# Turning the normalised rows by GpSimd and two-byte DMA transposes instead of TensorE, in six down stages of a macaron block

## The chip, the cores and the metric

The kernel runs on one NeuronCore of a Trainium2 chip. The metric is the device time of one execution in microseconds (us). The core has TensorE (PE in the profile; PEld is its loading of weights), VectorE (DVE), ScalarE (ACT), GpSimd (POOL) and SyncE (SP), which here issues nearly all DMAs. Each engine works through its own queue in order.

## The reference

The input is u, 2 x 1024 rows of 1024 numbers, in float32. The block is a feed-forward layer, an S4 layer (a long convolution along the row) and a second feed-forward layer, each on normalised rows and added to its input:

```
x = x + 0.5 * ffn(layernorm(x))
x = x + s4(layernorm(x))
x = x + 0.5 * ffn(layernorm(x))
ffn(x) = (silu(x @ Wg) * (x @ Wu)) @ Wd
```

Wg and Wu are 1024 x 2752, Wd is 2752 x 1024. They come as 4-bit integers with a scale and a zero point for every 128 rows. Both feed-forward layers use the same weights.

## The kernel before

The 2048 rows are cut into four blocks of 512 (TB), each of four tiles of 128 rows (NT = 4). With two feed-forward layers for each block there are eight jobs, in the order of the list `JOBS`: (block, layer) = (0,1), (1,1), (0,3), (1,3), (2,1), (3,1), (2,3), (3,3). Job j has two stages. `gate_up` takes 64 steps and computes silu(x Wg) * (x Wu); `down` takes 44 steps and multiplies by Wd. The last phases of a job overlap with the preparation of the next through hooks: lists of small functions, `up` and `dn`, that are called at a given step of the stage, before that step's matmuls are written. A scheduler then lays out each engine's queue; where `in_order_of_writing` wraps a hook, its instructions on the named engines keep the order in which they were written.

**Weights.** The integers minus their zero points were written to DRAM as bytes at the start. Every step needs one weight tile. `load_bytes` fetches its bytes by a DMA on SyncE (L627 for gate/up, L634 for down; written 4 steps ahead, 6 buffers), `make_weights` casts them to float32 on GpSimd (L643; written 3 steps ahead, 5 buffers). In a down step PE does eight matmuls of 128 x 512 (L758): four columns of the output, each with hidden values as a high part hh and a low part hl. After each step the sums in PSUM are scaled by the ratio of neighbouring scales, two of four by ScalarE (L665) and two by VectorE (L667). The products hh and hl of the last gate/up steps are still made by GpSimd (L727, L729) when the down stage begins.

**Rows into columns.** `gate_up` multiplies by the normalised rows with the features on partitions. It needs them in two pieces, named xTh (float32, 8 chunks x 512 rows) and xTl (float16, what the rounding of xTh left over). In the down stage of job j the pieces of job j + 1 are prepared, for its four row tiles t in turn:

- `normalized` (L221, VectorE): (x - mean) * 1/deviation, 128 x 1024, at step 1 + 4t.
- `turn` at steps 2 + 4t and 4 + 4t, for one half of 512 columns each: four PE transposes of 128 x 128 into a PSUM bank named pt (`turned`, L228), ScalarE copies them into xTh (L250), VectorE writes the difference as xTl (L251).

```
ps = turned(n, f"pt_{b}_{k}_{t}_{half}")
...
nc.scalar.copy(hi, ps)
nc.vector.tensor_tensor(lo, ps, hi.bitcast(F32), ALU.subtract)
```

In job 0 alone the copy goes to a buffer and GpSimd makes both pieces (L246 to L248), at steps that begin at 9. The pieces have one buffer each: the next job's are written while the down stage runs, after the present job's gate/up stage has read its own.

**Rows of the result.** From step 21 of a down stage `load_x` reloads the block's four row tiles from DRAM, and `back` (L780, L782) transposes the first half of the result by PE and adds it, at steps 26, 30, 34 and 38; the other half follows in the next gate/up stage. Row tiles of 128 x 1024 float32 of every kind share ten buffers (`t4`). Tiles g and hf have three buffers each and are otherwise used in gate/up stages.

Of the kernel before, what the change touches and what calls it, by code (L numbers as in the profile page):

```python
# [9 lines left out]
F32 = mybir.dt.float32  # L10
BF16 = mybir.dt.bfloat16
F16 = mybir.dt.float16
# [4 lines left out]
F32R = mybir.dt.float32r  # L17
AF = mybir.ActivationFunctionType
ALU = mybir.AluOpType
AX = mybir.AxisListType  # L20
ET = mybir.EngineType
# [3 lines left out]
P = 128  # L25
HID = 1024
INTER = 2752
TOK = 2048
TB = 512
NT = TB // P  # L30
NC = HID // P
# [24 lines left out]
def macaron_s4_kernel(  # L56
# [31 lines left out]
    nc = tc.nc  # L88
# [7 lines left out]
    xtpool = ctx.enter_context(tc.tile_pool(name="xT", bufs=1))  # L96
# [4 lines left out]
    gpool = ctx.enter_context(tc.tile_pool(name="g", bufs=3))  # L101
    hfpool = ctx.enter_context(tc.tile_pool(name="hf", bufs=3))
# [27 lines left out]
    def t4(name):  # L130
        return xpool.tile([P, HID], F32, tag="x", name=name)
# [9 lines left out]
    def in_order_of_writing(f, *engines):  # L141

        start = len(nc.cur_bb.bb.instructions)
        got = f()
        written = list(nc.cur_bb.bb.instructions)
        for e in engines:
            last = next((i for i in reversed(written[:start]) if i.engine == e), None)
            for ins in written[start:]:
                if ins.engine == e:
                    if last is not None:  # L150
                        tc.add_manual_dep(
                            ins,
                            last.name,
                            mybir.DependencyInfo(
                                mybir.DependencyClass.NoSync, mybir.DependencyReason.DATA
                            ),
                            reason="order of writing",
                        )
                    last = ins
        return got  # L160


    x = {}
    ln = {}

    def load_x(b, src):
        x[b] = []
        for t in range(NT):
            xt = t4(f"x_{b}_{t}")
            nc.sync.dma_start(xt, src[t])  # L170
            x[b].append(xt)

    def rows_of(dram, b):
        return [dram[bass.ds(b * TB + t * P, P), :] for t in range(NT)]

    def moments(b, k):
        for _ in moments_by_tile(b, k):
            pass

    def moments_by_tile(b, k):  # L180

        name = f"{b}_{k}"
        stats = small.tile([P, NT, 2, 6], F32, tag="stats", name=f"stats_{name}")
        mv = small.tile([P, NT, 2], F32, tag="mv", name=f"mv_{name}")
        for t in range(NT):
            for i in range(2):
                nc.vector.bn_stats(stats[:, t, i, :], x[b][t][:, bass.ts(i, 512)])  # L187
            nc.vector.bn_aggr(mv[:, t, :], stats[:, t, :, :].rearrange("p a s -> p (a s)"))
            yield
        guess(b, k, mv)  # L190
# [13 lines left out]
    def deviations(b, k, factor=1.0):  # L204


        mv, ve, r = ln.pop(b)
        e = small.tile([P, NT], F32, tag="e", name=f"e_{b}_{k}")
        for three in (3.0, 12.0, 768.0):
            nc.vector.tensor_tensor(e, r, r, ALU.mult)  # L210
            nc.vector.tensor_tensor(e, e, ve, ALU.mult)
            nc.vector.scalar_tensor_tensor(r, e, three, r, ALU.subtract, ALU.mult)
        nc.vector.tensor_scalar(r, r, -factor / 8192, None, ALU.mult)
        for t in range(NT):
            ln[b, t] = (mv[:, t, 0:1], r[:, t : t + 1], k)
        return r

    def normalized(b, t):
        m, r, k = ln[b, t]
        n = t4(f"xn_{b}_{k}_{t}")  # L220
        nc.vector.tensor_scalar(n, x[b][t], m, r, ALU.subtract, ALU.mult)  # L221
        return n

    def turned(n, name):

        ps = bank(name)
        for k in range(4):
            nc.tensor.transpose(ps[:, bass.ts(k, P)], n[:, bass.ts(k, P)], ident)  # L228
        return ps.rearrange("p (c t) -> p c t", c=4)


    pieces = {}

    def turn(b, t, n, half, by_pool=False):
        k = ln[b, t][2]
        if b not in pieces:
            pieces[b] = [
                xtpool.tile([P, NC, TB], dt, tag=f"xT{w}", name=f"xT{w}_{b}_{k}")
                for w, dt in (("h", F32R), ("l", F16))
            ]  # L240
        hi, lo = (a[:, 4 * half : 4 * half + 4, bass.ts(t, P)] for a in pieces[b])
        ps = turned(n, f"pt_{b}_{k}_{t}_{half}")
        if by_pool:
            both = gpool.tile([P, TB], F32, tag="g", name=f"turn_{b}_{k}_{t}_{half}")
            both = both.rearrange("p (c t) -> p c t", c=4)
            nc.scalar.copy(both, ps)  # L246
            nc.gpsimd.tensor_copy(hi, both)
            nc.gpsimd.tensor_tensor(lo, both, hi.bitcast(F32), ALU.subtract)  # L248
        else:
            nc.scalar.copy(hi, ps)  # L250
            nc.vector.tensor_tensor(lo, ps, hi.bitcast(F32), ALU.subtract)  # L251

# [275 lines left out]
    def in_pieces(at, hooks_and_steps, pieces):  # L530

        held = {}

        def piece(last):
            def step():
                if not held:
                    held[0] = pieces()
                for _ in held[0]:
                    if not last:
                        break  # L540

            in_order_of_writing(step, ET.DVE)

        for i, (hooks, s) in enumerate(hooks_and_steps):
            last = i == len(hooks_and_steps) - 1
            at(hooks, s, lambda last=last: piece(last))
# [114 lines left out]
    h = {}  # L661
# [128 lines left out]
    after = const.tile([P, 4, P], F32, tag="after", name="after")  # L790
# [227 lines left out]
    def s4_toeplitz():  # L1018

        rows, turn, whole = t4("s4_rows"), t4("s4_turn")[:, :P], t4("s4_whole")  # L1020
        nc.gpsimd.memset(turn, 0.0)
        nc.gpsimd.affine_select(
            out=turn,
            in_=turn,
            pattern=[[1, P]],
# [327 lines left out]
    def fast():  # L1353
        for j, (b, k) in enumerate(JOBS):
            prev = JOBS[j - 1] if j else None
            after = JOBS[j + 1] if j + 1 < len(JOBS) else None
            up, dn = {}, {}

            def at(hooks, s, f):
                hooks.setdefault(s, []).append(f)  # L1360

            if prev:
# [3 lines left out]
                if pk == 1:  # L1366
                    late = 34 if j == 1 else 0
# [51 lines left out]
            if j == 1:  # L1419
                tables = s4_tables()  # L1420
                for i in range(S4_PIECES):
                    piece = lambda: in_order_of_writing(lambda: next(tables, None), ET.DVE)
# [3 lines left out]
            if after:  # L1426
                ab, ak = after
                if ak == 1:
                    at(up, 55 if j == 0 else 6, lambda: load_x(ab, rows_of(u, ab)))
                    if j == 0:  # L1430
                        steps = [(dn, d) for d in range(3, 8)]
                        in_pieces(at, steps, lambda: moments_by_tile(ab, 1))
                        newton = lambda: deviations(ab, 1, LIFT)
                        at(dn, 8, lambda: in_order_of_writing(newton, ET.DVE))
                    else:
                        both = lambda: moments(ab, 1)
                        at(up, 44, lambda: in_order_of_writing(both, ET.DVE))
                        at(up, 45, lambda: deviations(ab, 1, LIFT))
                an = {}

                pool = j == 0

                def anorm(t):
                    an[t] = normalized(ab, t)

                o = 9 if j == 0 else 0
                for t in range(NT):
                    at(dn, o + 1 + 4 * t, lambda t=t: anorm(t))
                    at(dn, o + 2 + 4 * t, lambda t=t: turn(ab, t, an[t][:, :512], 0, by_pool=pool))
                    at(dn, o + 4 + 4 * t, lambda t=t: turn(ab, t, an[t][:, 512:], 1, by_pool=pool))  # L1450
# [6 lines left out]
        b = JOBS[-1][0]  # L1457
# [116 lines left out]
    srow_next, zeros_down = in_order_of_writing(start, *STARTING, ET.PE)  # L1574
    x.pop(0)
    fast()
    x.clear()
    other = nc.values_load(flag)
# [84 lines left out]
```

## Time and profile before

| | |
|---|---|
| three runs | 2132.9, 2134.52, 2134.49 us; median 2134.49 |
| profiled execution | 2136.97 us, span from first to last instruction 2135.1 us |
| granted TensorE clock | 0.997 |
| busy share of the span | PE 98%, DVE 80%, ACT 67%, POOL 50% |
| DMA | 132.14 MB, mean 62 GB/s |
| down stages of jobs 1 to 6 | 86.2, 85.5, 85.3, 85.6, 85.5, 85.4 us |
| down stage of job 7, until its last matmul | 81.6 us |
| gate/up stages of jobs 1 to 7 | 157.6 to 193.0 us |

A group in the profile is one line of code on one engine with its tiles: output <- inputs, with how often it ran, its busy time, the mean duration, and the idle time of that engine just before it, with what ended it. A releaser is what the engine was waiting for. Matmuls overlap in PE's pipeline, so a duration there is longer than the time from one start to the next. The stages' lengths are taken from the start of the first matmul of one stage (pg for gate/up, po for down) to that of the next.

### The profile page before, as it was taken

What the parts mean: (1) busy time and instruction counts of PE and PEld (TensorE: products, weight loads), DVE (VectorE), ACT (ScalarE), POOL (GpSimd) and SP (SyncE); (2) the same over time, 40 slices, a digit from 0 to 9 for tenths busy, and PEclk for the clock granted to TensorE, in tenths of its full rate; (3) what the DMA queues carried; (4) which work ended last, traced back from release to release, by engine and by line L of the source; (5) the groups of instructions that cost most, each with busy time, mean ns of one, the idle gap of its engine ahead of it and who ended that gap; (6) DMA issues with size and microseconds to landing.
All of it is one profiled execution on the core that took longest, in us unless ns stands there. A gap on an engine that the chain in (4) does not pass through costs nothing.

```text
span 2135.1 us, 30272 instructions
## 1 busy us (share of the span) xinstructions
PE 2087.0 (98%) x9748; PEld 1425.8 (67%) x9748; DVE 1702.1 (80%) x2781; ACT 1420.6 (67%) x2233; POOL 1072.9 (50%) x1438
## 2 busy tenths in 40 slices
PE   6999999999999999999999999999999999999997
PEld 4555665677776578665876568675686766866576
DVE  8988877778888777778777888878788787777776
ACT  6877777646655776676767766547775467767765
POOL 6867838743354643555335543455534545345632
PEclk9999999999999999999999999999999999999999
DMA  4434321112111211112121121112111131121111
GB/s 141 124 92 131 100 70 55 37 58 74 43 45 47 93 50 54 65 31 92 56 80 38 29 73 39 44 52 70 35 38 38 51 98 44 45 81 36 33 35 58
DMA packets 163110, 132.14 MB, mean 62 GB/s; under 512 B 22651, under 2 KB 150500, under 8 KB 162942
## 3 DMA queue, kind: packets, MB, share of 16 engines
q1 hardware_dynamic: 161926, 128.24, 19.7%
q8 instruction: 79, 1.29, 0.2%
q10 hardware_dynamic: 728, 1.29, 0.2%
q14 instruction: 89, 0.73, 0.1%
q0 software_dynamic: 288, 0.59, 0.1%
HBM read 104.45 MB, written 25.50 MB: 61 GB/s over the span
## 4 chain that ended last, share of the span: by engine, by line
PE 88%; DVE 6%; POOL 2%; DMA 1%; issue 1%; ACT 1%; SPq 0%; ACTq 0%; DVEq 0%; POOLq 0%
PE pg L695 53%; PE po L758 27%; PE pc L1084 3%; DVE pg L667 2%; PE pb L780 1%; PE pb L1084 1%; PE pt L228 1%; DVE po L667 1%; PE st L228 1%; DVE hf L725 1%; POOL q L551 0%; POOL qd L580 0%; POOL xTl L248 0%; DMA b<-wq 0%; POOL w_down L643 0%
## 5 line engine op out<-in xcount | busy, mean ns | idle before, releaser
L665 ACT ACTIVATE pg<-pg,rat 128x512 f32<-128x512 f32 x1240 | 787.1, 660 | 424.3 <-PE pg L695 423.2
L667 DVE TENSOR_TENSOR pg<-pg,rat 128x512 f32<-128x512 f32 x1168 | 776.9, 694 | 174.0 <-PE pg L695 170.0
L695 PE MATMUL pg<-xTh,w_up 128*128 128x512 f32 x2752 | 851.5, 438 | 2.7 <-DVE pg L667 1.7
L695 PE MATMUL pg<-xTl,w_up 128*128 128x512 f16 x2752 | 722.0, 382 | 8.5 <-POOL xTl L1518 3.2
L643 POOL CAST w_up<-b 128x768 fp32r<-128x768 int8 (+2 forms) x490 | 377.4, 776 | 519.0 <-PE pg L695 407.9
L695 PEld LDWEIGHTS pg<-xTh,w_up 128*128 128x128 f32 x2752 | 519.6, 189 | 176.8 <-DVE pg L667 14.9
L758 PE MATMUL po<-hl,w_down 128*128 128x512 f32 x1344 | 539.2, 403 | 9.5 <-DVE po L667 8.0
L665 ACT ACTIVATE po<-po,ratd 128x512 f32<-128x512 f32 x660 | 430.8, 662 | 159.0 <-PE po L758 159.0
L758 PE MATMUL po<-hh,w_down 128*128 128x512 f32 x1344 | 523.3, 392 | 0.0
L667 DVE TENSOR_TENSOR po<-po,ratd 128x512 f32<-128x512 f32 x620 | 427.4, 698 | 97.3 <-PE po L758 93.0
L695 PEld LDWEIGHTS <-w_up 128*128 128x128 bf16 x2752 | 228.1, 99 | 332.7 <-issue 156.2
L643 POOL CAST w_down<-bd 128x512 fp32r<-128x512 int8 x352 | 222.4, 634 | 410.2 <-PE po L758 338.6
L758 PEld LDWEIGHTS po<-hl,w_down 128*128 128x128 f32 x1344 | 251.9, 188 | 86.9 <-DVE po L667 21.9
L758 PEld LDWEIGHTS po<-hh,w_down 128*128 128x128 f32 x1344 | 252.8, 188 | 45.5
L729 POOL TENSOR_TENSOR hl<-hf,hh 128x512 fp32r<-128x512 f32 x168 | 220.1, 1310 | 7.9
L725 DVE SCALAR_TENSOR_TENSOR hf<-pg,rat,g 128x512 f32<-128x512 f32 x168 | 122.9, 748 | 45.5 <-ACT g L722 37.6
L722 ACT ACTIVATE g<-pg,rat 128x512 f32<-128x512 f32 x168 | 110.7, 687 | 49.2 <-PE pg L695 39.1
L727 POOL CAST hh<-hf 128x512 fp32r<-128x512 f32 x168 | 106.3, 633 | 55.5 <-PE pg L695 34.1
L187 DVE BATCH_NORM_STATS2 stats<-x 128x6 f32<-128x512 f32 x88 | 58.6, 677 | 0.5
L1114 DVE TENSOR_TENSOR x<-x,pc 128x512 f32<-128x512 f32 x32 | 22.0, 686 | 36.9 <-PE pc L1084 36.9
L1084 PEld LDWEIGHTS pc<-near,st 128*128 128x128 f32 x256 | 43.6, 190 | 7.9
L782 DVE TENSOR_TENSOR x<-x,pb 128x512 f32<-128x512 f32 x64 | 43.2, 679 | 6.2 <-PE pb L780 6.2
(210 smaller groups left out, 1049.7 us busy)
## 6 DMA issues: line engine op xcount, KB each, us to landing
b<-wq SPq DMA_DIRECT2D x319, 96.0 KB
bd<-wdq SPq DMA_DIRECT2D x336, 64.0 KB
x<-in_L_attn_u_dram SPq DMA_DIRECT2D x30, 512.0 KB
b<-wq SPq DMA_DIRECT2D x128, 64.0 KB
xs<-x SPq DMA_DIRECT2D x16, 512.0 KB
x<-xs SPq DMA_DIRECT2D x16, 512.0 KB
out_dram<-x SPq DMA_DIRECT2D x16, 512.0 KB
b<-wq SPq DMA_DIRECT2D x64, 80.0 KB
```

Source lines behind the costliest of these rows:

```text
L187: nc.vector.bn_stats(stats[:, t, i, :], x[b][t][:, bass.ts(i, 512)])
L643: nc.gpsimd.tensor_copy(t, b)
L665: nc.scalar.activation(dst, src, AF.Copy, scale=sc)
L667: nc.vector.tensor_tensor(dst, src, sc.to_broadcast([P, TB]), ALU.mult)
L695: nc.tensor.matmul(p, weights, (lo, hi)[k][:, g, :], start=(g == 0 and not done), stop=(g == GK - 1 and done), skip_group_check=True,)
L722: nc.scalar.activation(g, pg, AF.Silu, scale=rat[:, 2 * f, GK - 1 :])
L725: nc.vector.scalar_tensor_tensor(hf, pu, last, g, ALU.mult, ALU.mult)
L727: nc.gpsimd.tensor_copy(hi, hf)
L729: nc.gpsimd.tensor_tensor(lo, hf, hi.bitcast(F32), ALU.subtract)
L758: nc.tensor.matmul(ps[c], w[:, bass.ts(c, P)], part, start=(f == 0 and k == 0), stop=(f == NF - 1), skip_group_check=True,)
L782: nc.vector.tensor_tensor(part, part, ps, ALU.add)
L1084: nc.tensor.matmul(dst, lhsT, rhs, start=start, stop=stop, skip_group_check=True)
```

## The change

In the down stages of jobs 1 to 6 the rows are split before they are turned, and DMAs turn them. Job 0 keeps the old way; job 7 prepares nothing. A new function `turn_by_dma` is a generator that writes one piece of work at each call:

- VectorE normalises the tile in two halves of 512 columns.
- GpSimd, for each half: hi (n rounded to the matmul's float32) and top (n rounded to bfloat16); then mid = hi - top in bfloat16; then lo = n - hi in float16.
- SyncE issues three DMA transposes of 128 x 1024 two-byte elements: top and mid into a row-tile buffer named turned, lo straight into xTl.
- GpSimd adds the turned top and mid into xTh, in two halves of four chunks.

The pieces are hooked at steps 2 + 9t + d with d = 0, 1, 2, 3, 5, 6, 7, 9 and then 13 and 17 (12 and 13 for the last tile), each in order of writing on GpSimd and SyncE.

```diff
+    def turn_by_dma(b, t, after):
...
+        hi_t, lo_t = (a[:, :, bass.ts(t, P)] for a in pieces[b])
+        halves = [slice(0, 512), slice(512, HID)]
+        m, r, _ = ln[b, t]
+        n = t4(f"xn_{name}")
+        for own in halves:
+            nc.vector.tensor_scalar(n[:, own], x[b][t][:, own], m, r, ALU.subtract, ALU.mult)
+        yield
+        hi = t4(f"hi_{name}").bitcast(F32R)
+        top = hfpool.tile([P, HID], BF16, tag="hf", name=f"top_{name}")
+        mid = hfpool.tile([P, HID], BF16, tag="hf", name=f"mid_{name}")
+        lo = gpool.tile([P, HID], F16, tag="g", name=f"lo_{name}")
+        for own in halves:
+            nc.gpsimd.tensor_copy(hi[:, own], n[:, own])
+            nc.gpsimd.tensor_copy(top[:, own], n[:, own])
+            yield
+            nc.gpsimd.tensor_tensor(mid[:, own], hi[:, own].bitcast(F32), top[:, own], ALU.subtract)
+            yield
+            nc.gpsimd.tensor_tensor(lo[:, own], n[:, own], hi[:, own].bitcast(F32), ALU.subtract)
+            yield
+        both = t4(f"turned_{name}").bitcast(BF16).rearrange("p (i c t) -> p i c t", i=2, c=NC)
+
+        def transposes():
+            nc.sync.dma_start(both[:, 0], top, transpose=True)
+            nc.sync.dma_start(both[:, 1], mid, transpose=True)
+            nc.sync.dma_start(lo_t, lo, transpose=True)
+
+        transposes()
+
+        def sums():
+            for half in range(2):
+                own = slice(4 * half, 4 * half + 4)
+                nc.gpsimd.tensor_tensor(hi_t[:, own], both[:, 0, own], both[:, 1, own], ALU.add)
+                yield
+
+        after.append(sums())
...
-                for t in range(NT):
+                for t in range(NT if j else 0):
+                    late = (12, 13) if t == NT - 1 else (13, 17)
+                    for d in (0, 1, 2, 3, 5, 6, 7, 9) + late:
+                        piece = lambda t=t: turning(t)
+                        piece = lambda piece=piece: in_order_of_writing(piece, ET.Pool, ET.SP)
+                        at(dn, 2 + 9 * t + d, piece)
+                for t in range(0 if j else NT):
```

`turning(t)`, new as well, starts the generator of tile t at its first call and takes its next piece at each further one, the sums after the transposes.

More of the change, by code (lines that the diff above doesn't have):

```diff
@@ L251, in turn @@
             nc.vector.tensor_tensor(lo, ps, hi.bitcast(F32), ALU.subtract)
+    def turn_by_dma(b, t, after):
+        k = ln[b, t][2]
+        name = f"{b}_{k}_{t}"
+        if b not in pieces:
+            pieces[b] = [
+                xtpool.tile([P, NC, TB], dt, tag=f"xT{w}", name=f"xT{w}_{b}_{k}")
+                for w, dt in (("h", F32R), ("l", F16))
+            ]
+        hi_t, lo_t = (a[:, :, bass.ts(t, P)] for a in pieces[b])
[29 more added lines that the diff above has]
+        after.append(sums())
     UNITS = 2 * WIDE + 1
@@ L1446, in fast, with turning @@
                 o = 9 if j == 0 else 0
-                for t in range(NT):
+                turns = {}
+                def turning(t):
+                    if t not in turns:
+                        turns[t] = [], []
+                        turns[t] += (turn_by_dma(ab, t, turns[t][1]),)
+                    rest = turns[t][1] or turns[t][2:]
+                    next(rest[0], None)
+                for t in range(NT if j else 0):
[5 more added lines that the diff above has]
+                for t in range(0 if j else NT):
                     at(dn, o + 1 + 4 * t, lambda t=t: anorm(t))
```

## The prediction

> **What bounds the kernel now.** I read the page first (busy shares, then the chain of work that ended last), then a table of stretches for the down stages, then the timeline of one stage, then the GpSimd groups and the waits.
>
> ```profile
> PE 2087.0 (98%) x9748; PEld 1425.8 (67%) x9748; DVE 1702.1 (80%) x2781; ACT 1420.6 (67%) x2233; POOL 1072.9 (50%) x1438
> PE 88%; DVE 6%; POOL 2%; DMA 1%; issue 1%; ACT 1%; SPq 0%; ACTq 0%; DVEq 0%; POOLq 0%
> ```
>
> TensorE (PE) is busy 98% of the span and is 88% of the chain. Time that PE doesn't spend is time saved, if no other engine comes late. The table of stretches gives the six down stages that the change touches (488-574, 762-848, 1007-1093, 1254-1339, 1526-1611, 1797-1883 us) and the last one, which turns nothing. Two rows of all instructions, then two of the tile pt alone (columns: stretch, its length, then busy us and instruction count by engine):
>
> ```profile
> core 0: us, PE busy (x) PEld busy (x) DVE busy (x) ACT busy (x) POOL busy (x), PEclk, DMA share, GB/s
> 1525.60:1611.10 85.50, 85.09 (x395) 68.36 (x393) 69.10 (x104) 59.35 (x93) 31.84 (x48) 1.00 0.13 38
> 2040.40:2122.00 81.60, 81.32 (x362) 65.42 (x360) 63.30 (x92) 55.48 (x85) 28.76 (x44) 1.00 0.10 29
> ...
> 1525.60:1611.10 85.50, 5.11 (x32) 4.08 (x32) 5.52 (x8) 4.71 (x8) 1.00 0.13 38
> 2040.40:2122.00 81.60, 0.00 (x0) 0.00 (x0) 0.00 (x0) 0.00 (x0) 1.00 0.10 29
> ```
>
> The two stages have the same 344 down matmuls and 16 transposes of the result; the first has 32 pt transposes more, and is 3.9 us longer. PE is full in both. The timeline shows what a group of four costs:
>
> ```profile
> 1538.74 0.39 PE L758 MATMUL po<-hh,w_down 128*128 128x512 f32 x1
> 1538.97 0.60 PE L228 MATMUL pt<-ident,xn 128*128 128x128 f32 x4
> 1539.33 0.48 PE L758 MATMUL po<-hl,w_down 128*128 128x512 f32 x1
> 1539.64 0.39 PE L758 MATMUL po<-hh,w_down 128*128 128x512 f32 x1
> ```
>
> Matmuls start every 0.23 us. From 1538.97 to 1539.64 are 0.67 us for four transposes and one matmul, so four transposes cost 0.44 us, 0.11 us each, though each is 0.27 us long.
>
> GpSimd (POOL) has room in these stages, and these rows price what comes to it (busy, mean ns):
>
> ```profile
> L643 POOL CAST w_down<-bd 128x512 fp32r<-128x512 int8 x352 | 222.4, 634 | 410.2 <-PE po L758 338.6 <-PE pg L695 36.9 <-issue 21.2
> L727 POOL CAST hh<-hf 128x512 fp32r<-128x512 f32 x168 | 106.3, 633 | 55.5 <-PE pg L695 34.1
> L729 POOL TENSOR_TENSOR hl<-hf,hh 128x512 fp32r<-128x512 f32 x168 | 220.1, 1310 | 7.9
> L248 POOL TENSOR_TENSOR xTl<-turn,xTh 128x512 f16<-128x512 f32 x8 | 11.3, 1416 | 0.1
> POOL w_down L643 <- PE po L758: 338.6, 259, 2.3
> SPq L634 <- POOL w_down L643: 416.3, 277, 4.0
> ```
>
> The two last lines are waits (total, times, longest): GpSimd's cast of down weights waits for PE to free a weight buffer, and SyncE's load of bytes waits for the cast to free a byte buffer. Both run ahead as far as buffers let them: five weight tiles, so four steps of 1.83 us, 7.3 us; six byte tiles, so some six casts more, 11 us. That is the cover for a late GpSimd or a late queue.
>
> **What the Trainium skill says.** TensorE: Matmul & The Clock Gate, Part 4: a PE transpose took about 275 ns in a kernel; the trace agrees on the duration (272 ns), and shows that only 0.11 us of it is PE's time. GPSIMD Engine Reference, 3.1: a two-input operation is about 2.6 cycles an element, so an estimate of 1.1 us for 512 plus dispatch; the trace has 1.31 us. The same page, Specifications: the SBUF interfaces are shared with VectorE; the trace agrees, a w_down cast beside a VectorE row operation (L221) took 1.07 us at 489.4 instead of 0.62. VectorE: DVE Perf Modes, The three transpose paths: 1309 ns for 128x128 two-byte elements by DMA. No DMA transpose is in the trace of before.
>
> **The change part by part**, for each of six stages, four row tiles each.
>
> 1. *PE loses 32 transposes.* By the timeline 32 x 0.11 = 3.5 us; by stage lengths 4.6, 3.9, 3.7, 4.0, 3.9 and 3.8 over 81.6, together 23.9 us for six. The surplus is a short stall at the stage's start where PE waits for DVE (0.41 us at 1530.1), which the row normalisation, still on DVE, may keep. Ends 21.1 and 23.9; I take 22.5.
> 2. *DVE loses 8 subtractions (5.5 us), ACT 8 copies (4.7 us)* a stage. Neither bounds the stage (DVE 69 of 85.5): nothing. The row operation becomes two halves, the same 1.0 us and one more start.
> 3. *GpSimd gains ten operations a tile:* four casts x 0.633, four subtractions x 1.310, two strided sums x 1.416 (L248 is the nearest row; bf16 inputs are not in the trace). That is 2.5 + 5.2 + 2.8 = 10.6 us, 42.4 a stage; with the 31.8 of now 74.2 of 81.6 us. One tile has nine steps, 16.5 us: nine weight casts (5.5) and 10.6 make 16.1. It fits, barely. Two row halves on DVE can hold GpSimd 0.45 us each: 17.0, 0.5 late a tile, 2 us over four, inside the 7.3 us of lead. Value taken: nothing. Low end nothing, high end in the rival below. Behind a waiting piece stand the w_down casts, and PE behind these.
> 4. *SyncE gains 12 transposes a stage*, 72 in all, of 256 KB. The built order puts each behind one more byte load, top first, then mid, then lo, each waiting for its last GpSimd half; the loads behind it are held at most about two steps, 3.7 us, of 11. To issue a load takes SyncE 0.32 us (row of L634), so 3.8 us a stage if a transpose is as quick to issue.
> 5. *The transposes themselves.* Low: Advanced Engine Details and Errata, X-Bar Transpose, says nearly as fast as regular DMAs; DMA: Bandwidth & Descriptors, Latency, has 261 GB/s measured, its Anatomy 2.0 us fixed per DMA. Estimate: 256 KB / 261 GB/s = 1.0 us each in a row, 3 us to land. High: eight blocks x 1309 ns one after another = 10.5 us each. The first tile's second half is reached at step 7 (12.8 us), and two casts with a subtraction follow: the first transposes are ready some 15 us into the stage, so s us each ends at 15 + 12 s: up to s = 5.5 all are done within 81.6. The sums stand five weight casts behind the last mid, about 9 us at PE's pace; a landing of 3 to 5 us doesn't stop GpSimd. I take the low end, hidden.
> 6. *Buffers.* A tile now holds three x buffers of ten (normalised, hi, turned) where one was. At step 21, with four rows loaded back, I count 9. In the built order the last tile's normalisation waits for the first tile's second sum, which is due ten steps earlier. Nothing, unless GpSimd is that late. top and mid use the hf buffers, lo a g buffer; the next stage's first use is its step 7, some 15 us on.
>
> **Sum.** The profiled execution took 2136.97 us (span 2135.1): less 22.5 = 2114.5. The median of the three runs is 2.5 us below it: 2112.
>
> **Rivals.**
>
> *A, hidden:* 2112 as summed (2108 to 2125 with stalls of up to 2 us a stage at its seam). For it: the last stage, without any turning, is 81.6 us of full PE, and GpSimd's idle time in these stages (48.9 of 85.4 before w_down in the stage from 1797) is larger than what comes.
>
> *B, slower: the queue of transposes becomes the bound.* Place: the seam to the next gate/up stage, whose first matmul reads xTl of all four tiles. A stage then ends at 15 + 12 s. It pays for the saved 3.75 us at s = 5.9 and loses from there: s = 7 gives 99, that is 13.6 net a stage, +82, 2216; s = 10.5 gives 141, +334, 2468. For it: nothing in the trace shows such a DMA, and the 1309 ns is a single block. Against: two pages give near-copy rates.
>
> *C, slower: GpSimd becomes the bound* because operations on bf16 cost more than f32. Lag allowed is 7.3 us over four tiles, 1.8 a tile: from 12.8 us a tile, 21% above the price, PE waits. At 1.5 times: 15.9 + 5.5 = 21.4 against 16.5, four times 4.9 less 7.3 = 12.3 late, 8.5 net a stage: +51, 2185.
>
> *D, given back:* the w_down casts or the seam come 3.75 us late a stage, by part of B or C: 2130 to 2139.
>
> That the PE transposes stay is excluded: in the built order 192 of 256 pt transposes are gone.
>
> **Numbers.** A 0.74; D 0.05; B 0.15; C 0.06. A measurement of this kernel tells about 0.2%, 4.3 us, from no change. Faster 0.74, same 0.05, slower 0.21. The range runs from 2106 (all of the 23.9, and 0.8 us a stage of the stalls behind DVE at its start) to 2150, which takes in D and B up to s = 6.05 (15 + 72.6 = 87.6, so 6.0 late a stage, 36 on 2112); beyond lie some 0.17.
>
> **What would show it.** Right: down stages of 81.6 to 82.2 us, no pt rows there, POOL busy about 74 us in each with no PE wait for w_down or xTl; casts near 0.63, subtractions near 1.31; transposes landing within 5 us. Wrong: PE waiting at the first gate/up matmul for a DMA into xTl or for the sum into xTh (B), waiting for w_down inside the stage (C), or SyncE's loads late behind a transpose.

## The result, and the profile after

The kernel after takes 2125.54 us (median of five runs, 2125.37 to 2125.94) against 2134.52 for the kernel before (five runs, 2132.9 to 2136.98): a ratio of 0.9956, 95% interval 0.9942 to 0.9971. It is faster by 9.0 us, where 22.5 were forecast. The profiled execution took 2125.47 us (span 2123.6), 11.5 less than the one before.

The page's busy time of each engine, and the shares of the chain that ended last:

```profile
PE 2071.9 (98%) x9556; PEld 1405.8 (66%) x9556; DVE 1688.6 (80%) x2757; ACT 1396.8 (66%) x2185; POOL 1290.1 (61%) x1678
PE 88%; DVE 8%; ACT 1%; DMA 1%; issue 1%; POOL 1%; SPq 0%; ACTq 0%; DVEq 0%; POOLq 0%
```

TensorE lost its 192 transposes (9748 to 9556 instructions), GpSimd gained 217 us of work, and the chain is still TensorE's. But VectorE's share of the chain rose from 6% to 8%, though it does less work than before. That is the first hint.

The table of stretches of the kernel after (stretch, length, then busy us and instruction count by engine; last, the share of the DMA engines and what they moved), for two changed down stages and the unchanged last one:

```profile
core 0: us, PE busy (x) PEld busy (x) DVE busy (x) ACT busy (x) POOL busy (x), PEclk, DMA share, GB/s
759.70:843.40 83.70, 82.34 (x362) 65.08 (x360) 67.15 (x98) 55.42 (x85) 68.64 (x88) 1.00 0.48 126
1787.60:1871.30 83.70, 82.35 (x362) 65.13 (x360) 67.20 (x98) 55.47 (x85) 68.62 (x88) 1.00 0.48 126
2028.90:2110.50 81.60, 81.35 (x362) 65.44 (x360) 63.28 (x92) 55.50 (x85) 28.65 (x44) 1.00 0.10 29
```

All three have the same 362 matmuls, yet the changed stages are 2.1 us longer than the last. The six of them take 84.3, 83.8, 83.7, 83.9, 83.9 and 83.7 us (86.2, 85.5, 85.4, 85.6, 85.5 and 85.4 before; the third is 85.39, not the 85.3 of the table ahead), from the first matmul into po to the next stage's first into pg. Together they gained 10.1 us of the 11.5, and 13.7 us are left over 6 x 81.6. In the stage at 1787.6 TensorE is busy 82.35 of 83.70 us: it waits. The timeline of VectorE, of GpSimd and of TensorE, at one such wait:

```profile
1801.26 0.70 DVE L714 TENSOR_TENSOR po<-po,ratd 128x512 f32<-128x512 f32 x1 [0.21 <-PE po L805]
1801.87 0.54 DVE L269 TENSOR_SCALAR xn<-x,mv,r 128x512 f32<-128x512 f32 x1
1802.32 0.69 DVE L714 TENSOR_TENSOR po<-po,ratd 128x512 f32<-128x512 f32 x1
1802.92 1.37 DVE L269 TENSOR_SCALAR xn<-x,mv,r 128x512 f32<-128x512 f32 x1
1804.21 1.28 DVE L714 TENSOR_TENSOR po<-po,ratd 128x512 f32<-128x512 f32 x2
```

```profile
1802.85 1.16 POOL L279 TENSOR_TENSOR mid<-hi,top 128x512 bf16<-128x512 f32 x1
```

```profile
1804.01 0.39 PE L805 MATMUL po<-hh,w_down 128*128 128x512 f32 x1
1804.95 0.50 PE L805 MATMUL po<-hl,w_down 128*128 128x512 f32 x1 [0.56 <-DVE po L714]
```

L269 is the row normalisation, now in two halves; L714 multiplies a down result by its scale and so frees a PSUM buffer po. The first half takes 0.54 us. The second starts 0.07 us after GpSimd's subtraction mid (L279) and takes 1.37 us: mid ends 1.08 us after the half began, and the half 0.29 us later. The scaling behind it starts 1.29 us after this half began, where the one behind the free half started after 0.45 us: 0.84 us late. The matmul that needs the buffer starts 0.94 us after the one before instead of 0.23. In this stage the starts stand apart by 0.83 us too much for tile 1 (this gap and the next), 0.83 for tile 2 and 0.48 for tile 3: the 2.1 us. The waits of TensorE for the scaling (total, times, longest), after and then before:

```profile
PEld po L805 <- DVE po L714: 40.6, 80, 1.6
PE po L805 <- DVE po L714: 13.2, 25, 1.2
```

```profile
PEld po L758 <- DVE po L667: 21.9, 44, 1.6
PE po L758 <- DVE po L667: 8.0, 13, 1.2
```

Did these row operations stand in the down stage before? They were written there, but in the built order 20 of the 24 ran in the gate/up stages ahead; only the first of the six stages had its four rows in it, at its steps 0 to 7. The stretches of row operations alone (L221 before, L269 after; the first number behind the comma is VectorE's busy time), for the first and the sixth stage:

```profile
488.30:574.50 86.20, 3.53 (x4) 1.00 0.21 62
1797.40:1882.80 85.40, 0.00 (x0) 1.00 0.17 50
```

```profile
487.90:572.30 84.40, 6.95 (x8) 1.00 0.40 100
1787.60:1871.30 83.70, 5.47 (x6) 1.00 0.48 126
```

After, each tile holds three x buffers, and the built order has the halves of tiles 1 to 3 in the down stage, all at steps 7, 16 and 25, though they are written at 11, 20 and 29. Tile 0's still run in the gate/up stage, but for the first of the six stages.

What was new to GpSimd and SyncE came as priced or cheaper. First the GpSimd groups of the page (busy, mean ns), then the answers for single tiles (ns least/median/most, first and last start):

```profile
L281 POOL TENSOR_TENSOR lo<-xn,hi 128x512 f16<-128x512 f32 x48 | 61.7, 1286 | 0.0
L279 POOL TENSOR_TENSOR mid<-hi,top 128x512 bf16<-128x512 f32 x48 | 57.0, 1187 | 0.0
L295 POOL TENSOR_TENSOR xTh<-turned 128x512 fp32r<-128x512 bf16 x48 | 55.8, 1163 | 0.0
```

```profile
L269 DVE TENSOR_SCALAR xn<-x,mv,r x48: 527/791/1368, 488.6 to 1837.6; 128x512 f32<-128x512 f32 x48
L286 SPq DMA_TRANSPOSE turned<-top x24: 1232/1257/1378, 502.9 to 1853.7; - x24
L288 SPq DMA_TRANSPOSE xTl<-lo x24: 1231/1232/1247, 506.9 to 1857.7; - x24
```

The idle column of the sums L295 is 0.0: GpSimd never waited for a transpose to land. Against that, a row half's median is 0.79 us, not 0.54.

### The profile page after: what moved, and what is told of

Read it like the earlier page. It is cut to its first block, busy times and chain, and to the rows that moved or that the text cites. A ratio compares the mean times of both kernels' runs of the same rounds, so it can differ in the third digit from the quotient of the medians.

```text
span 2123.6 us, 30212 instructions
## 1 busy us (share of the span) xinstructions
PE 2071.9 (98%) x9556; PEld 1405.8 (66%) x9556; DVE 1688.6 (80%) x2757; ACT 1396.8 (66%) x2185; POOL 1290.1 (61%) x1678
## 3 DMA queue, kind: packets, MB, share of 16 engines
q10 hardware_dynamic: 728, 1.29, 0.2%
## 4 chain that ended last, share of the span: by engine, by line
PE 88%; DVE 8%; ACT 1%; DMA 1%; issue 1%; POOL 1%; SPq 0%; ACTq 0%; DVEq 0%; POOLq 0%
PE pg L742 56%; PE po L805 26%; PE pc L1131 3%; DVE po L714 2%; PE pb L827 1%; PE pb L1131 1%; DVE pg L714 1%; DVE xn L269 1%; PE st L228 1%; DVE hf L772 0%; DMA b<-wq 0%; DVE rawd L565 0%; POOL q L598 0%; DMA x<-in_L_attn_u_dram 0%; ACT g L769 0%
## 5 line engine op out<-in xcount | busy, mean ns | idle before, releaser
L714 DVE TENSOR_TENSOR pg<-pg,rat 128x512 f32<-128x512 f32 x1168 | 777.4, 693 | 179.8 <-PE pg L742 175.1
L805 PE MATMUL po<-hl,w_down 128*128 128x512 f32 x1344 | 535.9, 402 | 14.8 <-DVE po L714 13.2
L714 DVE TENSOR_TENSOR po<-po,ratd 128x512 f32<-128x512 f32 x620 | 428.7, 697 | 102.7 <-PE po L805 97.6
L281 POOL TENSOR_TENSOR lo<-xn,hi 128x512 f16<-128x512 f32 x48 | 61.7, 1286 | 0.0
L279 POOL TENSOR_TENSOR mid<-hi,top 128x512 bf16<-128x512 f32 x48 | 57.0, 1187 | 0.0
L295 POOL TENSOR_TENSOR xTh<-turned 128x512 fp32r<-128x512 bf16 x48 | 55.8, 1163 | 0.0
```

Source lines behind the costliest of these rows:

```text
L281: nc.gpsimd.tensor_tensor(lo[:, own], n[:, own], hi[:, own].bitcast(F32), ALU.subtract)
L714: nc.vector.tensor_tensor(dst, src, sc.to_broadcast([P, TB]), ALU.mult)
L805: nc.tensor.matmul(ps[c], w[:, bass.ts(c, P)], part, start=(f == 0 and k == 0), stop=(f == NF - 1), skip_group_check=True,)
```

## The experiments

Three theories stood at the start. V: VectorE's row halves are held by GpSimd's two-input operations, and the scaling behind them comes late. M: the mere move of the rows into the down stage costs, whatever GpSimd does. D: the DMA transposes, or GpSimd's traffic, slow the stage. Each edit below is against the kernel after, except where before is named.

### 1. No row operation (D)

```diff
-        n = t4(f"xn_{name}")
-        for own in halves:
-            nc.vector.tensor_scalar(n[:, own], x[b][t][:, own], m, r, ALU.subtract, ALU.mult)
+        n = x[b][t]
```

> Left out: the normalisation in the down stages of jobs 1 to 6; GpSimd splits the raw row tiles. All else as in the changed kernel. Theory V (VectorE's row halves, held while a two-input GpSimd operation runs, make the scaling late and PE waits): the stages of 83.7 us fall to that of job 7, 81.6 to 81.9; the execution to 2112 to 2114 us. Theory M (the move of the rows from the gate/up stage into the down stage costs, whatever runs beside): the same. Theory D (transposes by DMA and GpSimd's traffic slow TensorE or the scaling): stays at 83.7 and 2125.

Measured: 2110.39 us in one run. Its stretch of the stage that starts at 1774.7:

```profile
1774.70:1856.30 81.60, 81.35 (x363) 65.46 (x361) 63.27 (x92) 55.50 (x85) 67.98 (x88) 1.00 0.51 130
```

The six stages take 81.9, 81.6, 81.6, 81.7, 81.7 and 81.6 us. With every transpose and all of GpSimd's splitting in place, TensorE is as full as in the last stage. D is refuted: what is lost comes with the row halves. Leaving them out also takes away one row buffer a tile and the tie of GpSimd's casts to VectorE; experiment 2 keeps both.

### 2. Both halves held at their written steps (V against M)

```diff
-    piece = lambda piece=piece: in_order_of_writing(piece, ET.Pool, ET.SP)
+    piece = lambda piece=piece: in_order_of_writing(piece, ET.Pool, ET.SP, ET.DVE)
```

> The changed kernel with VectorE added to the engines in order of writing, so that a tile's two halves run at their written steps 2, 11, 20, 29, both in a row, instead of steps 7 and 16 beside the subtraction mid. V: each half 0.54 to 0.6 us, 1.1 us in a row, more than the 0.4 us that VectorE has free in a step but with no held half: stages 82.0 to 82.8, 2115 to 2119 us. M and D: 83.7, 2125.

Measured: 2114.71 us (2114.2 to 2115.14), ratio 0.9902 (0.9887 to 0.9918). Stages of 82.3, 82.1, 82.1, 82.1, 82.1 and 82.1 us. The tile's answer, and the waits:

```profile
L269 DVE TENSOR_SCALAR xn<-x,mv,r x48: 537/539/547, 492.9 to 1833.5; 128x512 f32<-128x512 f32 x48
```

```profile
PEld po L805 <- DVE po L714: 27.7, 63, 1.7
PE po L805 <- DVE po L714: 6.5, 12, 1.2
```

The same 48 halves of the same size, all 24 tiles' now in the down stage, take 0.54 us each, because at their written steps at most the last 0.04 us of a cast are left when one begins. Of the 13.7 us left over, 10.6 are gone. V is what this shows; M may keep 0.5 us a stage.

### 3. The halves a step apart

```diff
         for own in halves:
             nc.vector.tensor_scalar(n[:, own], x[b][t][:, own], m, r, ALU.subtract, ALU.mult)
-        yield
+            yield
...
-                    for d in (0, 1, 2, 3, 5, 6, 7, 9) + late:
+                    for d in (-1, 0, 1, 2, 3, 5, 6, 7, 9) + late:
...
-                        piece = lambda piece=piece: in_order_of_writing(piece, ET.Pool, ET.SP)
+                        piece = lambda piece=piece: in_order_of_writing(piece, ET.Pool, ET.SP, ET.DVE)
```

> As the pinned one, and the two halves of a tile a step apart (steps 1 and 2 + 9t), where GpSimd has only casts. V: halves of 0.54 us with at most 0.1 us of waiting each: stages 81.7 to 82.1, 2113 to 2115 us. M: above 83, 2122 or more. D: 83.7, 2125.

Measured: 2120.61 us (2119.34 to 2121.94), ratio 0.9927 (0.9914 to 0.9941). Stages of 82.9, 82.6, 82.5, 82.6, 83.2 and 83.1 us: a miss, as V's number was lower.

```profile
L269 DVE TENSOR_SCALAR xn<-x,mv,r x48: 537/750/1223, 495.1 to 1840.6; 128x512 f32<-128x512 f32 x48
```

Two halves issued together meet the end of one cast; two halves apart each meet an operation of their own. In the stage from about 1787 the second halves took 0.75 to 0.88 us, three of them beside casts and one beside the end of a sum, and one first half 1.22, which began 0.35 us after the subtraction lo (L281, 1.29 us long). V has to be widened: casts hold a half too, only for less long. Some 3 us of this run lie outside the changed stages: the first job's gate/up stage took 178.4 us, against 175.1 in the profile of experiment 2.

### 4. The kernel before, with its row operation moved into the down stage (M alone)

Against the kernel before:

```diff
+                own = (ET.DVE,) if j else ()
...
-                    at(dn, o + 1 + 4 * t, lambda t=t: anorm(t))
+                    moved = lambda t=t: anorm(t)
+                    at(dn, o + 1 + 4 * t, lambda moved=moved: in_order_of_writing(moved, *own))
```

> The kernel before, with the row operation (one of 128 x 1024) of jobs 1 to 6 held on VectorE at its written steps 1, 5, 9 and 13 of the down stage; in the kernel before it runs in the gate/up stage. No GpSimd two-input operation stands beside it but hl at the stage's start. M (the move costs by itself): stages from 85.5 to 87 or more, 2145 us or more. V (the held half costs, the move little): 0.8 us each with 0.4 us of slack a step, the first one longer beside hl: stages 85.6 to 86.4, 2135 to 2141 us. D says nothing of it.

Measured: 2138.31 us in one run, beside 2135.7 for before. Stages of 86.1, 85.9, 85.9, 86.0, 85.9 and 85.9 us, so 0.4 to 0.5 us a stage more than before in five of six. The other is the first, where the row operations stood in the down stage before as well. They took 0.80 to 0.81 us, but the first of each stage 1.01, with 0.46 us left of a cast when it began. Row operations that are hardly held cost little in the down stage. M is real but small.

### 5. The subtractions replaced by casts

```diff
-            nc.gpsimd.tensor_tensor(mid[:, own], hi[:, own].bitcast(F32), top[:, own], ALU.subtract)
+            nc.gpsimd.tensor_copy(mid[:, own], hi[:, own].bitcast(F32))
...
-            nc.gpsimd.tensor_tensor(lo[:, own], n[:, own], hi[:, own].bitcast(F32), ALU.subtract)
+            nc.gpsimd.tensor_copy(lo[:, own], near.rearrange("p a b -> p (a b)"))
```

> Left out: the two differences; mid is a cast of hi and lo a cast of a constant tile, 0.61 us each instead of 1.16 and 1.28 of two inputs. VectorE's order stays that of the changed kernel, halves at steps 7 and 16. V: the second halves fall from 1.37 us to 0.9 or less, stages to 82 to 82.6, 2115 to 2119 us. M: stays at 83.7. D: stays near 83.7, since the transposes are all there.

Measured: 2119.39 us in one run; stages of 83.2, 82.6, 82.6, 82.7, 82.7 and 82.5 us, at or a little above the upper end of V's number (82.6).

```profile
L269 DVE TENSOR_SCALAR xn<-x,mv,r x48: 526/742/878, 489.4 to 1831.6; 128x512 f32<-128x512 f32 x48
```

The halves stand where they stood, beside a GpSimd operation of 0.61 us instead of 1.16, and the held half takes 0.80 us instead of 1.37. What decides is how long the GpSimd operation still runs, not that it has two inputs.

### 6. One row operation of 128x1024, held at the written step

```diff
-        for own in halves:
-            nc.vector.tensor_scalar(n[:, own], x[b][t][:, own], m, r, ALU.subtract, ALU.mult)
+        nc.vector.tensor_scalar(n, x[b][t], m, r, ALU.subtract, ALU.mult)
...
-                        piece = lambda piece=piece: in_order_of_writing(piece, ET.Pool, ET.SP)
+                        piece = lambda piece=piece: in_order_of_writing(piece, ET.Pool, ET.SP, ET.DVE)
```

> The pinned kernel (row operation at steps 2, 11, 20, 29) with one operation of 128 x 1024 in place of two halves. By the rows of before it takes 0.80 us where two halves take 1.08. V: stages 81.8 to 82.1 instead of 82.1 and 2112 to 2115 us. M: as the pinned one. A fourth reading, that GpSimd must wait longer for its first half, gives 82.1 or more.

Measured: 2112.8 us (four runs, 2111.56 to 2116.71), ratio 0.9889 (0.9871 to 0.9907). Stages of 82.3, 81.8, 81.8, 82.2, 82.1 and 81.8 us.

```profile
L268 DVE TENSOR_SCALAR xn<-x,mv,r x24: 804/806/806, 496.4 to 1835.7; 128x1024 f32<-128x1024 f32 x24
```

One start fewer, 0.81 us instead of 2 x 0.54. By its median this is the fastest version with the row normalisation in it, and it beats both kernels; against experiment 2 the intervals overlap. Its profiled run is the one of 2116.71, with the first job's gate/up stage at 178.6 us, outside the change.

### 7. Held in order, but beside a subtraction

```diff
-                    for d in (0, 1, 2, 3, 5, 6, 7, 9) + late:
+                    for d in (-3 if t else 0, 1, 2, 3, 5, 6, 7, 9) + late:
...
-                        piece = lambda piece=piece: in_order_of_writing(piece, ET.Pool, ET.SP)
+                        piece = lambda piece=piece: in_order_of_writing(piece, ET.Pool, ET.SP, ET.DVE)
```

> The pinned kernel with the rows of tiles 1, 2 and 3 at steps 8, 17 and 26 instead of 11, 20 and 29, in order of writing all the same: there GpSimd works on the two differences of the tile before. V: halves of 1.0 us and more again, stages back to 83 to 84, 2120 to 2126 us. If the fixed order alone brought the gain: 82.1, 2115.

Measured: 2137.93 us in one run, beside 2135.7 for before. Stages of 86.3, 86.1, 86.1, 86.2, 86.2 and 86.1 us. The stretch of the sixth stage, then the timeline of VectorE (the two halves drawn as one line), GpSimd and TensorE at its tile 1:

```profile
1797.70:1883.80 86.10, 83.04 (x363) 64.97 (x361) 69.90 (x100) 55.31 (x85) 68.98 (x88) 1.00 0.46 123
```

```profile
1814.94 2.31 DVE L269 TENSOR_SCALAR xn<-x,mv,r 128x512 f32<-128x512 f32 x2
1817.17 1.28 DVE L714 TENSOR_TENSOR po<-po,ratd 128x512 f32<-128x512 f32 x2
```

```profile
1814.93 1.28 POOL L281 TENSOR_TENSOR lo<-xn,hi 128x512 f16<-128x512 f32 x1
1816.18 0.79 POOL L690 CAST w_down<-bd 128x512 fp32r<-128x512 int8 x1
```

```profile
1816.41 0.49 PE L805 MATMUL po<-hl,w_down 128*128 128x512 f32 x1
1817.91 0.50 PE L805 MATMUL po<-hl,w_down 128*128 128x512 f32 x1 [1.01 <-DVE po L714]
```

Both halves now meet a GpSimd operation one behind the other (1.55 and 0.83 us), and TensorE's starts stand 1.5 us apart at tiles 1 and 2 and 1.16 at tile 3. With the gaps that follow, these three places cost 4.2 of the 4.5 us by which this stage is longer than that of experiment 1. Three steps of placement, with nothing else changed, cost 4 us a stage against experiment 2 and all that the change gained. It is more than V's number, which counted on the size of hold seen in the kernel after. Holding the order is not what helped in experiment 2; where the halves stand is.

### 8. The rows on ScalarE

```diff
+        shift = small.tile([P, 1], F32, tag="moved", name=f"moved_{name}")
+        nc.vector.scalar_tensor_tensor(shift, m, -1.0, r, ALU.mult, ALU.mult)
         for own in halves:
-            nc.vector.tensor_scalar(n[:, own], x[b][t][:, own], m, r, ALU.subtract, ALU.mult)
-        yield
+            nc.scalar.activation(n[:, own], x[b][t][:, own], AF.Identity, bias=shift, scale=r)
+            yield
...
-                    for d in (0, 1, 2, 3, 5, 6, 7, 9) + late:
+                    for d in (-1, 0, 1, 2, 3, 5, 6, 7, 9) + late:
...
-                        piece = lambda piece=piece: in_order_of_writing(piece, ET.Pool, ET.SP)
+                        piece = lambda piece=piece: in_order_of_writing(piece, ET.Pool, ET.SP, ET.DVE, ET.Activation)
```

> The rows of jobs 1 to 6 by ScalarE instead of VectorE, in halves at steps 1 and 2 + 9t, after one small VectorE operation for the shift. ScalarE took 0.75 us for such a half at the start of the kernel, and has 0.5 us free in a step. V: nothing is held by GpSimd any more; ScalarE's scaling is up to 0.3 us late eight times: stages 81.6 to 82.5. If any further operation on a scaling engine costs its length, as M says: 83 or more.

Measured: 2119.22 us in one run; stages of 82.8, 82.9, 83.0, 83.2, 82.6 and 82.8 us. Better than the kernel after, but above V's number (82.5 at most); two stages reach M's 83. ScalarE's halves take 0.81 us each and stand ahead of its own scalings. The small operation left on VectorE costs too: in the sixth stage it takes 0.46 us (1788.25), and TensorE then waits twice for VectorE's scaling (0.39 and 0.19 us). Of the 1.0 us by which this stage is longer than in experiment 6, 0.6 are lost by step 6, where these waits lie; how the rest divides stays open.

## Why the prediction was wrong in size and right in kind

**The step that failed** is the second, "The row operation becomes two halves, the same 1.0 us and one more start", costed at nothing. It was argued from VectorE's average (69 of 85.5 us busy), and it took for granted that the halves stay where the row operation was and last as long. In fact the built order moved three tiles' halves into the down stage, and at tiles 1 and 2 the second half landed 0.07 us behind the start of mid and took 1.37 us. With the smaller holds of tile 3 that is 2.1 us a stage over the full 81.6, and 13.7 us over six stages. Experiment 2 gives back 10.6 us of stage time by placement alone; experiment 6, with the halves joined as well, 11.3.

The kernel before had shown the price. In its first down stage, the row operation of 0.80 us stood beside a GpSimd subtraction (timeline of VectorE, then of GpSimd):

```profile
235.33 1.79 DVE L221 TENSOR_SCALAR xn<-x,mv,r 128x1024 f32<-128x1024 f32 x1
```

```profile
234.83 1.74 POOL L248 TENSOR_TENSOR xTl<-turn,xTh 128x512 f16<-128x512 f32 x1
```

The prediction read only the other direction: a GpSimd cast that a row operation held from 0.62 to 1.07 us. That very row operation (L221 at 488.93) had itself taken 1.12 us instead of 0.80, behind another cast (L727).

The Trainium skill, SBUF — State Buffer, "SBUF: two separate sides", calls the port pair that the two engines share "an exclusive lock, not a bandwidth split": whichever starts first has it for its whole instruction, and the other waits. Of VectorE's operations it names those in a two-port mode and those with two SBUF inputs. The row operation has one tensor input, so it would have to be of the first sort, which no run here shows. The durations agree with a wait to the end of GpSimd's instruction. A half takes what is left of GpSimd's operation at its start, and then 0.28 to 0.29 us: 1.08 + 0.29 = 1.37 behind mid, 1.27 + 0.28 = 1.55 behind lo (experiment 7), 0.52 + 0.28 = 0.80 behind a cast (experiment 5), 0.94 + 0.28 = 1.22 (experiment 3). A row twice as long takes the rest and 0.55: the 1.79 us above are 1.24 left of L248 + 0.55, the 1.12 us are 0.57 left of L727 + 0.55. Free, a half takes 0.54 us; so a GpSimd operation that ends within the first 0.25 us costs nothing. The first half of tile 1 in the kernel after shows it: 0.24 us of a cast were left, and it took 0.54. That it is this lock is the page's word; the profile shows durations, not ports.

**Step 1** had the right size. With nothing held (experiment 1) the stages come to 81.6 to 81.9 us, 23.4 us under before; with the rows in place (experiment 6) it is 21.4, inside the step's 21.1 to 23.9. Experiment 6's median of 2112.8 us lies beside the forecast 2112, but that is another kernel: the mechanism was right, and one term was missing.

**Step 3** was right, a little dear: 68.6 us of GpSimd a stage where 74.2 were forecast, more than half of the difference because mid took 1.19 and the sums 1.16 us instead of 1.31 and 1.42. Rival C is refuted. But the work does not only cost GpSimd: what it fills, VectorE's row operations can run into.

**Steps 4 and 5**: a transpose takes SyncE 1.23 us to issue, not the 0.32 of a load, so 14.8 us a stage rather than 3.8. TensorE didn't wait for it: its weight loads waited 2.4 us in all for w_down, before and after, and GpSimd's sums stood at 0.0 idle. The low end, hidden, was right, and rival B is refuted. Its 3 us to land were not measured: no trace here has a transpose's time to landing, and the 2.0 us fixed per DMA stand in a section on DMAs that GpSimd issues, while SyncE issues these. **Step 6** is where the move may come from: the buffers were counted for whether they would stop anything, at nothing, and not for where the built order would then put the halves. Which of the buffers' order and GpSimd's fixed order moved them was not tried apart.

Rival D, the whole gain given back (2130 to 2139), did not come either, though experiment 7 shows that the row halves alone can bring it. The time lies inside the range of 2106 to 2150, close to the case "with stalls of up to 2 us a stage", which the prediction placed at the stage's seam. The stalls are in its middle and have another cause, so it is luck that this number comes so near.

## What to carry to other kernels

When work goes to GpSimd, list the VectorE operations that read and write SBUF in the same stage, see in the built order which GpSimd operation each stands beside, and add that operation's remaining time to it. Where TensorE waits for VectorE to free PSUM, this counts even if both engines have a fifth of their time free. Cheap cures are to place the row operation at the end of a short GpSimd operation and hold it there, and, for a little more, not to split it (experiments 2 and 6).

## What the runs showed of the hardware that was not expected

- A VectorE row half of 0.54 us took up to 1.55 us beside one GpSimd operation, and a 128x1024 row 1.79 instead of 0.80.
- A two-byte DMA transpose of 128x1024 holds SyncE for 1.23 us. Twelve a stage raised the DMA engines' share from 0.17 to 0.48 (stage from 762 before, from 760 after), and in experiment 1 TensorE's pace stayed that of the stage without them.
- GpSimd's sum of two bfloat16 tiles into float32 took 1.16 us, less than the subtraction of two float32 tiles into float16 (1.29 us).
